# A decoder layer in float32: self-attention's product by V in sixteen squares of the array, the memory's weights on another queue, and a rearranged end

## The chip, the cores and the metric

The kernel runs on one core of a Trainium2 chip. A core has a matrix engine (TensorE, PE in the profile, with its weight loads shown as PEld), a vector engine (VectorE, DVE), an activation engine (ScalarE, ACT), a general engine (GpSimd, POOL), a synchronisation engine that only issues transfers (SyncE, SP), and 16 DMA engines. Each engine works through its own instruction stream in order and waits on semaphores. PE writes only to PSUM, eight banks of 128 partitions x 512 float32; DVE and ACT read PSUM, POOL does not. Transfers can be issued from SP, ACT and POOL.

The metric is the device time of one execution in microseconds. Times are compared with the median of runs of the kernel before.

## The reference

The input is x of 8 x 256 x 1024 (batch, token, channel), float32 throughout. Three blocks follow each other, each with a residual and a layer normalisation after it:

```python
x = layernorm(x + self_attention(x))        # 32 heads of 32, 8 key/value heads, rope, causal
x = layernorm(x + cross_attention(x, ctx))  # 32 heads of 128, 8 key/value heads, rope by position, key mask
x = layernorm(x + memory(x))                # 256 slots, the best 8, softmax, gate
```

What matters here is the first. Queries, keys and values are products of x with 1024 x 1024, 1024 x 256 and 1024 x 256 matrices; four query heads share one key/value head.

```python
attn = softmax(q @ k.T / sqrt(32) + causal)   # 256 x 256 for each head
out  = attn @ v                               # 256 x 32 for each head
return out.reshape(256, 1024) @ wo.T
```

The memory block projects each token to 64 channels, scores it against 256 slots, keeps the best eight, mixes their values, and adds the result with a gate that depends on the logarithm of the token's variance and on its mean over all tokens.

## The kernel before, in words

**Self-attention** (`self_attention`, about 0 to 1247 us) goes in 64 steps, s = 0 to 63, eight for each batch b; step c of a batch treats four query heads of four different key/value groups, c // 4 choosing which four. Inside this part the orders of PE and POOL are those in which the code names the instructions; the orders of DVE, ACT and SP are set by a planner. A step does:

- `transposed` (L295, L300), four times: the softmax weights of one head, 128 queries by 3 x 128 entries (the causal half has been left out), are transposed by PE in three 128 x 128 pieces into a bank of their own, `tr`, and copied to SBUF by ACT.
- `scores(s+1)` (L260): eight products on four 32-row strips of the array, into the two PSUM tiles `sc`. Then DVE adds the mask and takes the maximum (L275), ACT takes the exponential with its sum (L280), DVE the reciprocal (L284), and ACT scales (L286).
- `query(s+2)` (L207) with its rope on DVE (L217 to L220).
- `others(s)`: the output projection of the batch before (`project_out`, L340, L345, with the normalisation L134 to L146), or the keys and values of the next batch (L207, L233), and `turn` (L359), which transposes the normalised rows for cross-attention.
- `weighted(s)` (L308, L313): the product by V, eight products with 128 rows and 32 columns each, so that four heads lie side by side in four column strips of the array, and one copy by DVE (L318).

Between these, in steps 4 to 59, stand four products of cross-attention's keys and values (`one`, L677 and L683), part of a scheme that makes each 2 x 2 block product from seven products instead of eight (`seven`). Its sums of weights are made by POOL (`sum_event`, L385 to L434), one or two events in a step, and stored in DRAM.

Weights come through nine rotating SBUF buffers of 4 KB a partition, `w4` (`weights`, L110), loaded on SP's queue. SP runs ahead as far as these buffers are free. The key and value matrices `wk` and `wv` of self-attention are loaded once and stay.

**Cross-attention** (about 1250 to 3413 us) has 128 steps of one head for 512 queries: scores (L785), softmax (L794 to L805), a transposition of the weights in 32 x 32 blocks by DVE (`xa_turned`, L819), the product by V on four row strips of the array (`xa_weighted`, L836), four copies by ACT (L844), and query and output products (L683, L889) in between. V is read back from DRAM so that each strip has its copy (L602, on POOL's queue). Here only PE's order is written out. `memory_setup` stands at its beginning: it loads the memory block's weights on SP's queue (L1056 to L1065) and puts four empty places and then its preparations into the list `fill`, from which each step takes two entries.

**The tail** (`tail`, from about 3413 us) projects the last output, does the memory block for the last four of the 16 row tiles (`memory_tile`), and finishes all tiles (`final`): a product (L1312), the gated sum with row sums (L1315), the mean on DVE (L1321), the squares on ACT (L1323), the reciprocal root on POOL (L1324, L1325), one more DVE operation (L1326), and the normalisation by DVE for odd and by ACT for even tiles (L1330, L1332), stored by POOL's queue (L1333).

PSUM: three banks `mm` and one `tr` beside the two `sc` tiles of two banks each. In cross-attention two more single banks replace part of `sc`.

## Time and profile before

| | us |
|---|---|
| median of three runs (lowest, highest) | 3523.22 (3518.35, 3524.01) |
| the profiled execution | 3526.79 |
| its span, first to last instruction | 3524.6 |

The mean granted clock of the profiled execution is 0.985. In a row of the timeline the columns are the start in us from the span's beginning, the length in us, engine, line, operation, tiles (out<-in), shape and count. In the answer by stretch they are the stretch, its length, then busy us and number of instructions for PE, PEld, DVE, ACT and POOL, the clock that PE was granted, the busy share of the DMA engines and GB/s. In a row of waits they are who waited for whom, us in total, times, and the longest. Ends of matrix products are modelled and overlap the next start; how long PE is held is read from one start to the next.

### The profile page before, as it was taken

The numbers are of one execution on the slowest core, as the hardware profiler recorded it, in microseconds if no ns is written. First come the engines' busy times: TensorE is split into PE (matmuls) and PEld (weight loads), VectorE is DVE, ScalarE is ACT, GpSimd is POOL, SyncE is SP. The second block draws the span as 40 slices with busy tenths as digits, with TensorE's granted clock in tenths as the row PEclk, the third lists the DMA queues.
The fourth block names the chain that finished last, engine by engine and source line by source line (L and its number), as shares of the span: only waits on it lengthen the run. The fifth ranks groups of instructions, "written<-read, shape, count | busy, mean of one in ns | idle before, by whom it ended". The sixth has DMA issues, their size and how long they took to land.

```text
span 3524.6 us, 60801 instructions
## 1 busy us (share of the span) xinstructions
PE 3422.1 (97%) x22947; PEld 2472.4 (70%) x22947; DVE 2000.9 (57%) x5595; ACT 1287.0 (37%) x4139; POOL 1016.3 (29%) x1344
## 2 busy tenths in 40 slices
PE   7999999999999889999999999999999999999997
PEld 5777778777778657777676767766767776766763
DVE  3444444444444445655666566667566667566566
ACT  4544444444444423233323332323322333333224
POOL 3344555555656101211112111212111122111112
PEclk9999999999999999999999999999999999999997
DMA  6466777776766545444544444544444454444342
GB/s 246 165 212 210 260 251 235 242 244 211 261 230 213 170 149 172 142 127 144 162 142 147 136 131 133 162 143 149 137 132 127 152 162 134 142 130 133 132 150 96
DMA packets 233475, 600.52 MB, mean 170 GB/s; under 512 B 28832, under 2 KB 66016, under 8 KB 231904
## 3 DMA queue, kind: packets, MB, share of 16 engines
q1 hardware_dynamic: 159408, 411.32, 35.5%
q0 software_dynamic: 51712, 161.53, 13.7%
q10 hardware_dynamic: 22064, 23.79, 2.0%
q8 instruction: 183, 3.00, 0.3%
q14 instruction: 108, 0.88, 0.1%
HBM read 503.86 MB, written 92.67 MB: 169 GB/s over the span
## 4 chain that ended last, share of the span: by engine, by line
PE 90%; DVE 4%; ACT 2%; DMA 2%; issue 1%; POOL 1%; SPq 0%; POOLq 0%; ACTq 0%; DVEq 0%
PE mm L683 23%; PE mm L889 17%; PE mm L207 8%; PE mm L340 6%; PE mm L677 6%; PE sc L785 6%; PE mm L836 6%; PE tr L683 3%; PE tr L889 3%; PE tr L295 3%; PE mm L1165 2%; PE sc L260 2%; PE mm L233 1%; PE tr L836 1%; PE mm L308 1%
## 5 line engine op out<-in xcount | busy, mean ns | idle before, releaser
L683 PE MATMUL mm<-x1T,w 128*128 128x256 f32 x2976 | 712.8, 383 | 15.1 <-DMA w<-in_xa_wq 14.6
L683 PEld LDWEIGHTS mm<-x1T,w 128*128 128x128 f32 x2976 | 564.3, 191 | 169.3 <-issue 84.4
L799 ACT ACTIVATE xatt<-xatt,nmax 128x256 f32<-128x256 f32 x512 | 257.2, 503 | 499.6 <-DVE nmax L794 491.3
L889 PE MATMUL mm<-w,xoS 128*128 128x512 f32 x832 | 380.3, 596 | 0.9 <-issue 0.9
L602 POOL DMA_DIRECT2D v<-v x256 | 150.9, 596 | 739.2 <-PE mm L836 577.5
L300 ACT COPY at<-tr 128x384 f32<-128x384 f32 x253 | 121.1, 479 | 462.4 <-PE tr L295 462.4
L889 PE MATMUL mm<-w,xoT 128*128 128x512 f32 x620 | 284.1, 596 | 5.4 <-ACT xoT L844 4.1
L689 DVE TENSOR_TENSOR raw<-mm,half 128x256 f32<-128x256 f32 x339 | 141.6, 418 | 253.0 <-PE mm L683 154.7
L855 POOL TENSOR_TENSOR xoS<-xoT 128x512 f32<-128x512 f32 x62 | 79.1, 1276 | 700.1 <-ACT xoT L844 699.7
L689 DVE TENSOR_TENSOR half<-mm,half 128x256 f32<-128x256 f32 x256 | 107.3, 419 | 301.1 <-PE mm L683 249.8
L836 PEld LDWEIGHTS mm<-xat,v 32*128 32x128 f32 x6800 | 240.8, 186 | 42.5 <-issue 22.9
L889 PEld LDWEIGHTS mm<-w,xoS 128*128 128x128 f32 x832 | 154.9, 190 | 163.4 <-issue 144.2
L836 PE MATMUL mm<-xat,v 32*128 32x128 f32 x6800 | 265.8, 276 | 1.7 <-DVE rec L803 1.0
L785 PE MATMUL sc<-kT,qT 128*128 128x256 f32 x1024 | 264.2, 381 | 0.0
L805 ACT ACTIVATE xatt<-xatt,rec 128x256 f32<-128x256 f32 x512 | 231.0, 499 | 87.7 <-DVE rec L803 86.4
L280 ACT ACTIVATE att<-att,nmax 128x128 f32<-128x128 f32 (+1 forms) x512 | 225.5, 442 | 96.2 <-DVE nmax L275 96.2
L385 POOL TENSOR_TENSOR ws<-ws 128x256 f32<-128x256 f32 x320 | 240.8, 752 | 26.7 <-DMA ws<-in_xa_wk 6.2
L207 PE MATMUL mm<-xT,w 128*128 128x256 f32 x1024 | 245.6, 394 | 0.0
L844 ACT COPY xoT<-mm 128x128 f32<-128x128 f32 x425 | 88.9, 276 | 411.3 <-PE mm L836 287.3
L677 PE MATMUL mm<-w,ctxT 128*128 128x128 f32 x1792 | 224.6, 279 | 7.5 <-DMA w<-xa_wv_sums 3.1
L207 PEld LDWEIGHTS mm<-xT,w 128*128 128x128 f32 x1024 | 195.1, 196 | 48.4 <-issue 20.4
L340 PE MATMUL mm<-sa_wo,sa_oT 128*128 128x512 f32 x512 | 225.0, 592 | 0.0
(286 smaller groups left out, 5853.5 us busy)
## 6 DMA issues: line engine op xcount, KB each, us to landing
w<-xa_wq_sums SPq DMA_DIRECT2D x128, 512.0 KB, 3.6
w<-xa_wo_sums SPq DMA_DIRECT2D x124, 512.0 KB, 3.5
w<-in_xa_wo SPq DMA_DIRECT2D x97, 512.0 KB, 3.7
w<-in_sa_wq SPq DMA_DIRECT2D x64, 512.0 KB, 5.1
sa_wo<-in_sa_wo SPq DMA_DIRECT2D x64, 512.0 KB, 4.8
w<-in_xa_wq SPq DMA_DIRECT2D x64, 512.0 KB, 3.8
v<-v POOLq DMA_DIRECT2D x256, 128.0 KB
w<-xa_wk_sums SPq DMA_DIRECT2D x32, 512.0 KB, 7.0
```

The lines of the kernel that those rows point to most:

```text
L207: nc.tensor.matmul(ps[:, :S], lhsT=lhs[:, k, :], rhs=xT[:, k, :], start=(k == 0), stop=(k == KC - 1),)
L280: nc.scalar.activation(att[:, jj, lo:hi], att[:, jj, lo:hi], AF.Exp, bias=nmax[:, i : i + 1], scale=-1.0, accum_out=sums[:, i : i + 1],)
L340: nc.tensor.matmul(ps, lhsT=oTs[b * KC + c][:, tt * P : (tt + 1) * P], rhs=wos[b, half][c // 2][:, c % 2, :], start=(c == 0), stop=(c == K ...
L385: nc.gpsimd.tensor_tensor(out, in0, in1, op)
L677: nc.tensor.matmul(ps[:, t * P : (t + 1) * P], lhsT=rhs[:, k, t * P : (t + 1) * P], rhs=w[:, k, :], start=(k == 0), stop=(k == 3),)
L683: nc.tensor.matmul(ps[:, :S], lhsT=w[:, k, :], rhs=rhs[:, k, :], start=(k == 0), stop=(k == 3))
L689: nc.vector.tensor_tensor(out, in0, in1, ALU.add)
L785: nc.tensor.matmul(sc[:, qt, :], lhsT=qT[:, q0 : q0 + P], rhs=kT[:, b * S : (b + 1) * S], start=True, stop=True,)
L799: nc.scalar.activation(att[:, qt, :], att[:, qt, :], AF.Exp, bias=nmax[:, qt : qt + 1], scale=-1.0, accum_out=sums[:, qt : qt + 1],)
L805: nc.scalar.activation(att[:, qt, :], att[:, qt, :], AF.Identity, bias=0.0, scale=rec[:, qt : qt + 1])
L836: nc.tensor.matmul(banks[i][:, :P], lhsT=v[rows, c, :], rhs=at[rows, c, :], start=(c == 0), stop=(c == BLOCKS - 1),)
L889: nc.tensor.matmul(ps, lhsT=oT[lhs][:, u, off + p * P : off + (p + 1) * P], rhs=w[:, u, :], start=(u == 0), stop=(u == 1),)
```

## The change

1. **Product by V.** The transposes by PE and the product in four column strips go. After the softmax of a head DVE transposes it in 32 x 32 blocks into one tile `at` for two steps (even and odd s), and the product is made once for the two steps together: 104 products with 32 rows (keys) and 32 columns (channels of one head) each, on the sixteen 32 x 32 squares of the array. Each strip of 32 rows treats one block i of 32 queries out of each 128, against its own copy of V; the eight key blocks k follow one another and are summed in the strip's bank, one of four. The causal zeros are left out by block, so 40 of the 104 have 128 columns and 64 have 64. The product stands at the odd step, in two bursts, before the query and after the others. Its results lie in the two `sc` tiles. Four copies by ACT take them to SBUF.
2. **V by way of DRAM.** `values` stores V's rows in DRAM on ACT's queue, and `load_values` reads each half back four times, once for each strip, on SP's queue.
3. **Key and value weights** are no longer kept, but loaded for each batch through the `w4` buffers.
4. **Order.** Scores of odd steps come at the beginning of the step before them, those of even steps at the end, after the second burst. Query weights are asked for three steps ahead and output weights at steps 6 and 1 of a batch; the normalisation after the output projection is done one step later; the tables' transposes come at a step's end. The bank `tr` becomes a fourth `mm`. The `sc` tiles are given up one step later.
5. **Memory.** `memory_setup` runs at cross-attention's second step, its loads stand on POOL's queue, and two empty places remain of four. Tiles for the first query heads and the first softmax get their places early.
6. **End.** A scaling of the slot weights goes from DVE to ACT; the variance is written before the normalisation, and the last tiles' normalisation goes to ACT; two of the early `final` calls go to the end; in `final` the mean and the last factor go to POOL, the stores to SP's queue, and the last tile is normalised and stored in two halves.

```diff
-        self.banks = [(self.pool("mm", 3, space=PSUM), "mm")] * 3
-        self.banks_tr = [(self.pool("tr", 1, space=PSUM), "tr")]
+        self.banks = [(self.pool("mm", 4, space=PSUM), "mm")]
...
+        def load_kv(b, name):
+            for i in range(2):
+                src = a[name][:, :, i * P : (i + 1) * P] if name == "sa_wk" else a[name][:, 4 * i : 4 * i + 4, :]
+                wkvs[b, name, i] = self.weights([P, *src.shape[1:]], src)
...
-            nc.scalar.copy(vs[b][:, tt, :], ps[:, :256])
+            rows = sp.tile([P, SA_KV * SA_D], F32, name="sa_vrow", bufs=2)
+            nc.scalar.copy(rows, ps[:, :256])
+            if tt == 0:
+                v_d[b] = self.dram.tile([S, SA_KV * SA_D], F32, name=f"sa_v_{b}")
+            nc.scalar.dma_start(out=v_d[b][tt * P : (tt + 1) * P, :], in_=rows)
...
+            if s % 2 == 0:
+                ats[s // 2] = sp.tile([P, 4, 12, 2, 32], F32, name="at")
+            at = ats[s // 2]
...
+                for jj in range(2):
+                    turned = at[:, 2 * h + jj, :, s % 2, :]
+                    nc.vector.transpose(
+                        turned[:, :8].rearrange("p (c t) q -> p t c q", t=2),
+                        att[:, jj, :256].rearrange("p (t c q) -> p t c q", t=2, q=32),
+                    )
+                    nc.vector.transpose(turned[:, 8:], att[:, jj, 256:].rearrange("p (c q) -> p c q", q=32))
+
+        def load_values(b, half):
+            v = vs[b, half] = sp.tile([P, BLOCKS, 4 * SA_D], F32, name="sa_v", bufs=2)
+            rows = v_d[b].rearrange("(c i) d -> i c d", i=32)[:, :, half * P : (half + 1) * P]
+            for i in range(4):
+                nc.sync.dma_start(out=v[32 * i : 32 * i + 32], in_=rows)
...
+        def weighted(s, rest):
+            b, c = divmod(s, KC)
+            at, v = ats[s // 2], vs[b, c // 4]
+            if not rest:
+                pos[s] = [p_sc.tile([P, 2, 512], F32, name="sc") for _ in range(2)]
+            banks = [pos[s][i // 2][:, i % 2, :P] for i in range(4)]
+            for k in range(3, BLOCKS) if rest else range(3):
+                for i in range(max(k - 4, 0), 4):
+                    rows = slice(32 * i, 32 * i + 32)
+                    for j in range(4):
+                        lo, block = (0, slice(2 * k, 2 * k + 2)) if k <= i else (
+                            64, slice(2 * k + 1, 2 * k + 2) if k < 4 else slice(k + 4, k + 5)
+                        )
+                        nc.tensor.matmul(
+                            banks[i][32 * j : 32 * j + 32, lo:], lhsT=v[rows, k, 32 * j : 32 * j + 32],
+                            rhs=at[rows, j, block].rearrange("p x u q -> p (x u q)"),
+                            start=(k == 0), stop=(k == 4 + i),
+                        )
...
+            for i in range(4):
+                nc.scalar.copy(
+                    oT.rearrange("p u (t i q) -> p i t u q", t=2, i=4)[:, i],
+                    banks[i].rearrange("p (t u q) -> p t u q", t=2, u=2),
+                )
...
+            if s % 2:
+                weighted(s, False)
+            elif not first:
+                one()
+            if s % 2 == 0 and s + 1 < last:
+                scores(s + 1)
             if s + 2 < last:
                 query(s + 2)
+            while norms:
+                norms.pop(0)()
             for part in others(s):
                 part()
-            weighted(s, ats)
+            event()
+            one()
+            if s % 2:
+                weighted(s, True)
+                if s + 1 < last:
+                    scores(s + 1)
+            if c < 2:
+                load_values(b, c)
+            elif c == 6:
+                load_out(b, 0)
+            if b and c == 1:
+                load_out(b - 1, 1)
+            if s + 3 < last:
+                load_query(s + 3)
             while mine:
                 one()
...
-        self.memory_setup()
...
+            if H == 1:
+                self.memory_setup()
...
-            nc.sync.dma_start(out=t, in_=a[name] if src is None else src)
+            nc.gpsimd.dma_start(out=t, in_=a[name] if src is None else src)
...
-            nc.vector.tensor_scalar(w, w, rec, None, ALU.mult)
+            nc.scalar.activation(w, w, AF.Identity, bias=0.0, scale=rec)
...
-        nc.vector.tensor_scalar(nmean, sums[:, 0:1], sums[:, 1:2], -root / E, ALU.add, ALU.mult)
+        nc.gpsimd.tensor_tensor(nmean, sums[:, 0:1], sums[:, 1:2], ALU.add)
+        nc.gpsimd.tensor_scalar(nmean, nmean, -1.0 / E, None, ALU.mult)
...
-        nc.vector.scalar_tensor_tensor(nmr, nmean, 1.0 / root, rstd, ALU.mult, ALU.mult)
+        nc.gpsimd.tensor_tensor(nmr, nmean, rstd, ALU.mult)
...
-        finals(NT - 7)
+        finals(NT - 5)
```

## The prediction

> **What bounds the kernel now.** I read the shares of the engines first, then busy time by stretch, then TensorE's (PE's) timeline inside one step of self-attention, and its waits.
>
> ```profile
> PE 3422.1 (97%) x22947; PEld 2472.4 (70%) x22947; DVE 2000.9 (57%) x5595; ACT 1287.0 (37%) x4139; POOL 1016.3 (29%) x1344
> ```
>
> ```profile
> 480.00:640.00 160.00, 158.00 (x1033) 122.16 (x1032) 76.42 (x283) 76.19 (x254) 87.24 (x116) 1.00 0.73 243
> ...
> 1200.00:1240.00 40.00, 27.73 (x176) 20.22 (x173) 19.32 (x73) 21.68 (x76) 4.26 (x3) 0.80 0.65 232
> 1240.00:1320.00 80.00, 69.86 (x321) 47.24 (x323) 34.28 (x85) 18.47 (x57) 7.52 (x14) 0.92 0.43 132
> 1320.00:1760.00 440.00, 437.93 (x3180) 312.13 (x3176) 265.69 (x636) 141.27 (x467) 72.81 (x85) 1.00 0.46 150
> ...
> 3490.00:3525.00 35.00, 15.53 (x36) 6.52 (x35) 21.28 (x80) 18.80 (x29) 14.56 (x33) 0.63 0.47 190
> ```
>
> The columns after the length are PE, weight loads, DVE, ACT, POOL, the granted clock, the DMA share and GB/s. PE is full in self-attention (to about 1247) and in cross-attention (to about 3413). Only the joint between them (1200 to 1320) and the tail show gaps. So time is won by taking work off PE, or gaps out of the joint; work given to DVE is free as long as PE does not wait for it.
>
> Inside one step:
>
> ```profile
> 672.88 0.64 PE L308 MATMUL mm<-at,sa_v 128*32 128x256 f32 x8
> 673.33 0.40 PE L313 MATMUL mm<-at,sa_v 128*32 128x128 f32 x8
> 673.66 2.05 PE L677 MATMUL mm<-w,ctxT 128*128 128x128 f32 x16
> 675.55 0.49 PE L295 MATMUL tr<-ident,att 128*128 128x128 f32 x3
> 675.88 1.95 PE L677 MATMUL mm<-w,ctxT 128*128 128x128 f32 x16
> ...
> 1732.10 2.07 PE L836 MATMUL mm<-xat,v 32*128 32x128 f32 x64
> 1734.10 1.99 PE L683 MATMUL mm<-x1T,w 128*128 128x256 f32 x8
> ```
>
> Starts matter, since ends overlap. Three transposes hold PE from 675.55 to 675.88, 0.33 us; the product by V from 672.88 to 673.66, 0.78 us. The last two lines are cross-attention's product by V on four row strips, the nearest thing to the new one: 64 passes in 2.00 us.
>
> **The change, part by part.** The sum is made against the profiled execution, 3526.8 us (span 3524.6), which is 3.6 us over the median of 3523.2.
>
> *Work taken off PE.* Each of 64 steps loses four groups of transposes and one product: 4 x 0.33 + 0.78 = 2.10 us, in all -134 us. All of it is on the path.
>
> *The new product.* A pair of steps has 104 products in two bursts (48, then 56), each two passes in float32, like every product here (L836: 32 products, 64 passes): 208 passes. 40 products stream 128 columns and 64 stream 64. In L836's burst each strip starts a pass every 0.112 us (the timeline's rounds are 0.11 apart), the four strips of a round within 0.02 us, 6.7 ns apart. If sixteen squares run side by side as four strips do, a round of sixteen takes max(0.112, 16 x 6.7 ns) = 0.11 us a pass. First burst: three rounds of two passes, 0.67 us. Second burst: rounds of 16, 16, 12, 8 and 4 squares, 0.22 + 0.21 + 0.16 + 0.12 + 0.12 = 0.83 us. L836's 2.00 us is 16 x 0.112 = 1.79 plus 0.2 for turning the array over; I take 0.3 a burst since the first start also comes late. That is 2.1 us a pair, +67 us. Below: columns alone, (80 x 0.107 + 128 x 0.053)/16 = 0.96 us plus 0.4, +44. Above: nothing shows PE starting more than L836's 64 passes in 2.00 us over a whole burst; at 31 ns a pass, 208 take 6.5 us, +208. I take the low value, because L308 shows four column squares and L836 four row strips at that spacing, and L836's 31 ns is explained by its columns. A rule in the Trainium skill speaks against this: "TensorE: Matmul & The Clock Gate", section Back-to-back issue gap, gives a floor of about 25 ns between starts however few columns, and "TensorEngine Tiling (Array Packing)", section Instruction Overhead, warns against small dimensions for that reason. By it the bursts would be 208 x 25 ns + 0.6 = 5.8 us a pair, an estimate of +186 us; the starts 6.7 ns apart say that it does not hold between squares, but no run here shows sixteen.
>
> *The results share the scores' PSUM.* After the second burst the next scores wait until ACT has copied four 128x128 results:
>
> ```profile
> 1703.96 0.43 ACT L844 COPY xoT<-mm 128x128 f32<-128x128 f32 x2 [6.53 <-PE mm L836]
> 1704.28 0.28 ACT L844 COPY xoT<-tr 128x128 f32<-128x128 f32 x1
> 1704.43 0.30 ACT L844 COPY xoT<-mm 128x128 f32<-128x128 f32 x1
> ```
>
> There the last copy ends 0.86 us after PE's next work started (1703.87). In the new order the first strips end some 0.3 us before the last, and entering scores costs time anyway, so I take 0.4 us a pair, +13; bounds 0.2 and 1.2, +6 to +38.
>
> *Waits in self-attention.*
>
> ```profile
> PE tr L295 <- ACT at L300: 21.0, 32, 1.5
> PE mm L683 <- DMA w<-in_xa_wq: 13.1, 2, 9.9
> PE mm L295 <- ACT att L286: 6.2, 1, 6.2
> PE tr L295 <- ACT att L286: 3.9, 1, 3.9
> ```
>
> The first, third and fourth go with the transposes: -31. New: an odd step's first burst needs the whole softmax of scores issued in the step before. In the step of 682 scores end on PE at 683.26 and the last L286 at 690.36, 7.1 us later; the last head's DVE transposes add about 0.7. So 7.8 us must be covered. A step with four products of the next attention offers a query (3.65), three products (1.8 each) and an output projection (6.87) or keys or values (3.6): 12.6 to 15.9 us, enough. Steps without these products (0 to 3, 60 to 63) offer 2.6 to 7.3. I take 6 at step 61, 8 at 63 (DVE is held there by x1T's four 1024-wide operations), 3 at the start: +17. Net -14; bounds -25 and +5.
>
> *DVE* gets eight transposes a step. L819 gives 0.707 us for 128x512, and DVE's other 256- and 128-wide operations 0.42 and 0.28, so 4 x 0.70 = 2.8 us, less the removed 0.41 us copy (L318). Around 660 to 702.6 DVE is busy 19.5 of 42.6 us, 9.7 a step; then 12.1 of some 18.7, 65%. Cross-attention runs at 60% (265.7 of 440) with PE 99.5% busy, so I price it nearly at nothing. ACT loses four 0.48 us copies a step and gains two of 0.28.
>
> *DMA.* Key and value weights are fetched for every batch through the nine w4 buffers (+14.7 MB), V goes to DRAM by ACT's queue and comes back four times by SP's (+10.5 MB): 25 of 600 MB, with a share of 0.73 in the busiest stretch. Behind SP's wait for V stand query and product weights; a step of some 19 us between the write and its use covers it. Keys' weights in 512-byte rows may delay the start by 2 us. With DVE: +8; bounds 0 and +30. Deferred normalisations end a DVE wait for POOL that PE never felt: nothing. Output weights are asked for one or two steps earlier, and PE waits for none of them now (no row): nothing. Table transposes and POOL's sums change place inside a step; POOL is 55% busy there (87.2 of 160) and covers it.
>
> *The joint.* SP, in order, issues:
>
> ```profile
> 1286.22 0.65 SPq L1063 DMA_DIRECT2D m_in<-in_m_wu  x1
> ...
> 1299.05 0.49 SPq L1056 DMA_DIRECT2D m_gate_bias<-in_m_gate_bias  x1
> 1299.59 0.97 SPq L110 DMA_DIRECT2D w<-in_xa_wq  x2
> ```
>
> Query weights stand behind the memory's loads, and PE waits 9.95 us until 1306.16. On POOL's queue, a step later, they hold nothing that PE needs at once: -10. POOL's own V reloads (L602) stand behind twelve issues of 0.6 us, 7 us, with a pair of steps in hand. The router's turn comes after two empty places instead of four: if its weights are late, +4. Bounds -12 and +5.
>
> *The tail* is DVE's (26.8 of 30 us from 3460). It loses four scalings (0.35) and 32 one-column operations (about 0.15): -6; gains 1.5 normalisations (0.8), and two final tiles (1.4 each) move from DVE's idle time at 3453 to 3460 to the end: +4. POOL's longer chain per tile (five operations of 0.2 to 0.55) is shorter than DVE's 1.5 us and ACT's 1.3. Net -2; bounds -6 and +5. Other tile places and the order of banks (six in turn before and after): nothing, +-3.
>
> Sum: -134 + 67 + 13 - 14 + 8 - 10 - 2 = -72. 3526.8 - 72 = 3454.8; less 3.6, 3451 against the median.
>
> **Rivals.** *Slower: PE cannot start passes that fast.* At L836's 31 ns a pass the bursts cost 208 instead of 67: -72 + 141 = +69, 3592. It decides from the burst time where the -72 is gone: (67 + 72)/32 = 4.3 us a pair, 18 ns a pass after turning. For it: no sustained rate here is higher. Against: L836 is bound by columns.
>
> *Four at a time.* Squares of one strip, or of one column, take turns: (80 x 0.112 + 128 x 0.058)/4 + 0.6 = 4.7 us a pair, +150: -72 + 83 = +11, 3534. Against it: L308 streams four different right sides through the same rows.
>
> *The burst waits for DVE or ACT.* If in-order DVE holds the last blocks 1 us longer than covered, every pair pays 1 us, +32, 3483; 2 us, 3515. For it: where rope work came between, scores to last L286 took up to 9.4 us instead of 7.1, and DVE's load rises by a quarter. Against it: 4 to 8 us of cover in most steps.
>
> **How the numbers follow.** Forecast (3422 to 3475) 0.55; waits for DVE, ACT or DMA (3475 to 3515) 0.20; four at a time (3515 to 3545) 0.11; slow starts (over 3545) 0.10; better than 3422 0.04. A measurement tells 0.2%, 7 us, from no change. Slower takes 0.10 and 0.07 of the four-at-a-time case, same the other 0.04, faster 0.79. The range runs from 3422 to 3530 and leaves out about 0.2.
>
> **What the next profile would show.** Right: groups of form 32*32 with some 6650 passes, 2.1 us a pair in two bursts; no L295 or L300; idle under 0.5 us before the scores of even steps; DVE some 180 us busier; no 9.9 us wait for in_xa_wq; 625 MB moved. Wrong: bursts over 4 us, PE idle before first bursts in steady steps (released by DVE's transposes), or PE waiting for DMA of w or V.

## The result and the profile after

The changed kernel takes 3505.07 us in the median of five runs (3502.96 to 3509.42), the kernel before 3522.71 beside it (3518.35 to 3524.01): ratio 0.9958, 95% interval 0.9947 to 0.9969. The profiled execution took 3504.15 us, its span is 3502.4 against 3524.6. So the change is faster, by 18 us in the medians and 22 in the spans, where -72 was forecast. The time lies in the range, in the band of the rival "the burst waits for DVE or ACT" (3475 to 3515); whether it lies there for that reason is what the experiments were for.

The shares of the engines on the page of the changed kernel:

```profile
PE 3388.1 (97%) x27811; PEld 2459.2 (70%) x27811; DVE 2113.6 (60%) x5997; ACT 1201.2 (34%) x4030; POOL 1030.2 (29%) x1385
```

PE has 34 us less to do and 4864 passes more; DVE has 113 us more, not the 180 foreseen (the new transposes take 160, and the copy that goes, which the 180 left out, took 26), ACT 86 less. The stretches that answer to those shown of before:

```profile
480.00:640.00 160.00, 153.56 (x1610) 121.15 (x1610) 90.14 (x321) 58.51 (x217) 86.43 (x115) 0.96 0.76 255
1200.00:1240.00 40.00, 24.45 (x297) 17.49 (x298) 23.45 (x72) 14.55 (x54) 3.78 (x2) 0.79 0.55 197
1240.00:1320.00 80.00, 77.76 (x520) 55.53 (x519) 41.92 (x115) 25.41 (x82) 19.32 (x32) 1.00 0.59 190
1320.00:1760.00 440.00, 438.71 (x3067) 310.92 (x3066) 264.99 (x627) 136.75 (x451) 68.21 (x78) 1.00 0.47 147
3467.00:3502.00 35.00, 13.93 (x27) 5.34 (x26) 19.00 (x52) 17.75 (x28) 15.64 (x53) 0.64 0.47 187
```

In self-attention (first row) PE stands still for 6.4 of 160 us instead of 2.0, and the granted clock fell from 1.00 to 0.96. The joint (third row) is full now. The last 35 us have DVE busy for 19.0 us instead of 21.3, and POOL for a little more.

One step's timeline on PE:

```profile
646.19 1.49 PE L333 MATMUL sc<-at,sa_v 32*32 32x128 f32 x96
647.60 3.72 PE L208 MATMUL mm<-xT,w 128*128 128x256 f32 x16
651.16 7.03 PE L367 MATMUL mm<-sa_wo,sa_oT 128*128 128x512 f32 x16
658.03 1.89 PE L741 MATMUL mm<-ctxT,w 128*128 128x256 f32 x8
659.85 1.39 PE L333 MATMUL sc<-at,sa_v 32*32 32x64 f32 x112
661.34 1.35 PE L267 MATMUL sc<-sa_kT,sa_qT 32*128 32x128 f32 x16
```

From start to next start the two bursts (L333) hold PE for 1.41 and 1.49 us, 2.9 a pair instead of 2.1. And PE's waits up to 1320 us, the largest of them:

```profile
PE sc L333 <- DVE at L300: 18.5, 9, 12.4
PE mm L208 <- DMA xT<-in_xT: 10.2, 1, 10.2
PE sc L267 <- ACT sa_oT L343: 8.8, 8, 1.2
PE mm L735 <- DMA w<-xa_wv_sums: 7.8, 2, 5.8
PE sc L333 <- DMA sa_v<-sa_v: 6.1, 1, 6.1
PE mm L741 <- DMA w<-in_xa_wq: 3.8, 2, 1.9
PE mm L741 <- DMA w<-xa_wk_sums: 3.4, 1, 3.4
```

Where the 22 us of the spans lie, by the starts of the same work in both traces: cross-attention's first scores come at 1251.9 instead of 1268.1 (-16.2); from there to its first product by V 35.4 us instead of 47.7 (-12.3, the joint); to its last product by V 2099.8 instead of 2097.3 (+2.5); from there to the end 115.3 instead of 111.5 (+3.8). So the joint did what was said, the end a little worse, and nearly all that is missing, 44 us of the forecast's -60, is missing in self-attention.

### The profile page after: what moved, and what is told of

The parts are those of the page before. It is cut to its first block, busy times and chain, and to the rows that moved or that the text cites. A ratio compares the mean times of both kernels' runs of the same rounds, so it can differ in the third digit from the quotient of the medians.

```text
span 3502.4 us, 71117 instructions
## 1 busy us (share of the span) xinstructions
PE 3388.1 (97%) x27811; PEld 2459.2 (70%) x27811; DVE 2113.6 (60%) x5997; ACT 1201.2 (34%) x4030; POOL 1030.2 (29%) x1385
## 3 DMA queue, kind: packets, MB, share of 16 engines
q1 hardware_dynamic: 194672, 441.00, 38.6%
q8 instruction: 221, 3.62, 0.4%
## 4 chain that ended last, share of the span: by engine, by line
PE 71%; POOL 8%; issue 6%; DMA 6%; DVE 6%; ACT 2%; SPq 0%; POOLq 0%; ACTq 0%; DVEq 0%
PE mm L741 23%; PE mm L947 20%; PE mm L894 7%; PE sc L843 6%; PE mm L208 4%; POOL ws L417 3%; PE mm L735 3%; PE mm L367 2%; PE mm L1226 2%; DMA xa_wo_sums<-ws 2%; DMA xa_wq_sums<-ws 2%; PE sc L333 1%; PE sc L267 1%; POOL xa_wo_sums L466 1%; PE mm L1002 1%
## 5 line engine op out<-in xcount | busy, mean ns | idle before, releaser
L741 PE MATMUL mm<-x1T,w 128*128 128x256 f32 x3584 | 851.1, 381 | 5.0 <-DMA w<-in_xa_wq 3.8
L741 PEld LDWEIGHTS mm<-x1T,w 128*128 128x128 f32 x3584 | 676.3, 190 | 190.7 <-issue 87.7
L947 PE MATMUL mm<-w,xoS 128*128 128x512 f32 x992 | 449.2, 595 | 1.2 <-issue 1.2
L947 PE MATMUL mm<-w,xoT 128*128 128x512 f32 x744 | 338.2, 597 | 5.3 <-ACT xoT L902 4.1
L947 PEld LDWEIGHTS mm<-w,xoS 128*128 128x128 f32 x992 | 185.0, 190 | 194.2 <-issue 173.5
L208 PE MATMUL mm<-xT,w 128*128 128x256 f32 x1280 | 301.9, 392 | 10.2 <-DMA xT<-in_xT 10.2
L208 PEld LDWEIGHTS mm<-xT,w 128*128 128x128 f32 x1280 | 244.3, 195 | 59.9 <-issue 23.7
L747 DVE TENSOR_TENSOR raw<-mm,half 128x256 f32<-128x256 f32 x384 | 158.8, 414 | 153.0 <-PE mm L741 118.1
L947 PEld LDWEIGHTS mm<-w,xoT 128*128 128x128 f32 x744 | 138.7, 190 | 147.7 <-issue 126.8
L735 PEld LDWEIGHTS mm<-w,ctxT 128*128 128x128 f32 x1792 | 213.7, 197 | 24.9 <-issue 17.2
```

What stands on the lines that cost most here:

```text
L208: nc.tensor.matmul(ps[:, :S], lhsT=lhs[:, k, :], rhs=xT[:, k, :], start=(k == 0), stop=(k == KC - 1),)
L735: nc.tensor.matmul(ps[:, t * P : (t + 1) * P], lhsT=rhs[:, k, t * P : (t + 1) * P], rhs=w[:, k, :], start=(k == 0), stop=(k == 3),)
L741: nc.tensor.matmul(ps[:, :S], lhsT=w[:, k, :], rhs=rhs[:, k, :], start=(k == 0), stop=(k == 3))
L747: nc.vector.tensor_tensor(out, in0, in1, ALU.add)
L947: nc.tensor.matmul(ps, lhsT=oT[lhs][:, u, off + p * P : off + (p + 1) * P], rhs=w[:, u, :], start=(u == 0), stop=(u == 1),)
```

## The experiments

All runs are compared by their ratio to the kernel before on the same chip. A difference between two ratios, times 3522, is given in us; it is uncertain by some 6 us, so small effects are read from stages of the trace. "Alone" means one edit on the changed kernel.

### Every round of squares twice

```diff
-            for k in range(3, BLOCKS) if rest else range(3):
+            for rep, k in [(r, k) for k in (range(3, BLOCKS) if rest else range(3)) for r in range(2)]:
...
-                            start=(k == 0), stop=(k == 4 + i),
+                            start=(k == 0 and rep == 0), stop=(k == 4 + i and rep == 1),
```

> The changed kernel with every round of squares gone through twice: for each key block k the squares of all strips, then the same ones again, summed into the same bank. 208 more passes a pair of steps, 6656 in all; the output is not the layer's, since the product by V counts twice. It measures what a pass costs when nothing else is added. The prediction's size: rounds of sixteen at 0.11 us, so 1.5 us more a pair, +48 us over the changed kernel's 3505. My theory now (TensorE starts squares only every 11 to 12 ns once a burst has run for 32 passes, as read between starts in the trace after: 790 ns for 64 passes and 853 ns for 79): 208 x 10.8 to 12.3 ns = 2.25 to 2.56 us a pair, +72 to +82 us. Rival (self-attention is bound there by GpSimd's sums of weights or by the transfers, and TensorE's work is partly hidden): under +25 us.

3797.75 us, ratio 1.0781 (1.0764 to 1.0797): +290. PE's timeline of a pair without a pause inside:

```profile
660.74 2.73 PE L333 MATMUL sc<-at,sa_v 32*32 32x128 f32 x192
663.40 3.72 PE L208 MATMUL mm<-xT,w 128*128 128x256 f32 x16
...
675.70 2.58 PE L333 MATMUL sc<-at,sa_v 32*32 32x64 f32 x224
678.26 1.03 PE L267 MATMUL sc<-sa_kT,sa_qT 32*128 32x128 f32 x7
```

Thirteen first bursts and eight second ones without such a pause took 2.665 and 2.57 us on average, so 208 more passes cost 1.25 + 1.07 = 2.32 us, 11.1 ns each. That is what the trace after had said (2.25 to 2.56), +74 us for 32 pairs; 7.2 ns a pass, as forecast, falls, and so does the thought that PE's work is hidden there. The other 216 us no theory had. They are waits, most of them without a releaser (113 us more up to cross-attention's first scores), and a lower clock behind them (100 us; mean granted clock 0.951 instead of 0.982):

```profile
PE sc L333 <- issue: 126.2, 42, 4.9
```

### The 104 products in one burst

```diff
             if s % 2:
-                weighted(s, False)
-            elif not first:
+            if s % 2 == 0 and not first:
                 one()
...
             if s % 2:
+                weighted(s, False)
                 weighted(s, True)
```

> The changed kernel with the 104 products in one burst at the end of the odd step, where the second one stood, instead of two. Theory A (the bursts that come first wait for the softmax of the step before: the row of waits for DVE's transposes gives 18.5 us in nine times, 12.4 of them in the last step; and every burst pays once for turning over and filling): a turn of 0.25 us saved 32 times, -8, and 5 to 16 us of waits gone: -10 to -24 us, 3481 to 3495 us. Theory B (the waits come from work that is late anyway and turn up at the next place): -8 at most, and the last step's 12 us stay.

3580.76 us, ratio 1.0161 (1.0147 to 1.0175): +72, on the other side of both theories. The waits for the softmax did shrink (the row for DVE's transposes fell from 18.5 to 5.5 us), and a burst costs 2.80 us instead of 2.90. But there is the same new wait, 20 times in bursts and some times behind them, with a granted clock of 0.968:

```profile
PE sc L333 <- issue: 68.2, 20, 5.2
```

PE's timeline of this kernel:

```profile
648.47 2.70 PE L333 MATMUL sc<-at,sa_v 32*32 32x128 f32 x208
651.27 1.35 PE L267 MATMUL sc<-sa_kT,sa_qT 32*128 32x128 f32 x16
652.55 2.39 PE L734 MATMUL mm<-w,ctxT 128*128 128x128 f32 x19
657.47 5.02 PE L734 MATMUL mm<-w,ctxT 128*128 128x128 f32 x29 [2.54 <-issue]
```

PE stops in the middle of 48 like products whose weights and inputs are there. Its instructions are not: the answer on DMA traffic for 652 to 658 us of the same run has one packet of instructions,

```profile
q1 hardware_dynamic: 2077, 1.09, 87.4%
q0 software_dynamic: 154, 0.51, 25.0%
q8 instruction: 1, 0.02, 1.4%
```

and over the whole run 221 of them with 3.62 MB, 16 KB each. The 27,811 matrix instructions and as many weight loads are 252 to a packet, with PE's semaphore instructions 256.5; so they come in blocks of 256. In the trace's records this packet starts at 654.58 and takes 1.37 us; PE goes on 1.5 us after its end. Of the pauses of over 1.3 us between like instructions before 1290 us, 23 have this form: each ends with the same instruction of a block (numbers 193 and 194, modulo 256, semaphore instructions counted) and 1.25 to 1.6 us after a packet has landed. All 43 waits of over 1 us without a releaser in the doubled kernel's self-attention end with these two numbers too. A burst of 208 passes uses 416 instructions in 2.8 us, where products of 128 columns, 0.112 us from start to start, need 128 x 0.112 = 14.3 us for 256, and the next block isn't there in time. With bursts of 96 and 112 passes (192 and 224 instructions with their loads) and 12 us of other work between them, as in the timeline above, the kernel after has no pause of this form of over 1 us. The prediction took the two bursts for a matter of order; they are what keeps PE supplied.

### 128 columns everywhere

```diff
                         lo, block = (0, slice(2 * k, 2 * k + 2)) if k <= i else (
-                            64, slice(2 * k + 1, 2 * k + 2) if k < 4 else slice(k + 4, k + 5)
+                            0, slice(2 * k, 2 * k + 2) if k < 4 else slice(k + 3, k + 5)
```

> The changed kernel with 128 columns in all 104 products of a burst instead of 64 in 64 of them: the same number of instructions, 64 columns more in 128 of 208 passes. The extra columns take wrong blocks, so the output is not the layer's. If the number of instructions sets the rate: 128 passes of 0.11 us on sixteen squares are 7 ns each, under the 11 to 12 ns between starts, so nothing in the full rounds; the two short rounds at the end (8 and 4 squares, two passes each) grow by up to 0.2 us, 0 to +6 us over the changed kernel. If columns set it (64 columns at 0.055 us and 128 at 0.11, and the rate is set by squares waiting for one another): 128 x 0.055/16 = 0.44 us a pair at least, with the short rounds 0.6 to 1.0, +14 to +32 us.

3515.6 us, ratio 0.9980 (0.9968 to 0.9992): +8. First bursts kept their 1.415 us, though a quarter of their products have twice the columns now; second ones grew from 1.49 to 1.85. In the 1.49 are 0.10 us in which the scores behind the burst wait for the copies; the 1.85 have no such wait, so the burst itself grew by 0.46 us. That is over the 0.2 allowed where only instructions count, and at the lower end of the 0.44 to 1.0 where only columns do; the +8 us in all are under the 14 to 32 of that case, as the waits for the copies fell by 6 us. What tells most is the difference between the bursts: in each round of the first (one pass of all squares of a key block) some square had 128 columns already, in four of the five key blocks of the second none had. The longest square of a round counts, and it counts in full: eight rounds x 0.053 us = 0.43, against 0.46 measured.

### Four steps in one product

```diff
-            if s % 2 == 0:
-                ats[s // 2] = sp.tile([P, 4, 12, 2, 32], F32, name="at")
+            if s % 4 == 0:
+                ats[s // 4] = sp.tile([P, 4, 12, 4, 32], F32, name="at")
...
-                att = sp.tile([P, 2, 384], F32, name="att", bufs=3)
+                att = sp.tile([P, 2, 384], F32, name="att", bufs=2)
...
-            banks = [pos[s][i // 2][:, i % 2, :P] for i in range(4)]
+            banks = [pos[s][i // 2][:, i % 2, : 2 * P] for i in range(4)]
...
-            oT = sp.tile([P, 2, S], F32, name="sa_oT", bufs=6)
+            oT = sp.tile([P, 4, S], F32, name="sa_oT", bufs=2)
...
-            if s % 2:
+            if s % 4 == 3:
                 weighted(s, False)
...
```

> The changed kernel with the product by V made once for four steps instead of two: 104 products of 256 and 128 columns, so half the instructions for the same columns; one tile of transposed weights for four steps, the output of self-attention in tiles of four steps (two of them), and two buffers instead of three of the softmax weights, to make room. If the number of instructions costs the time: two bursts of 2.9 us become one of 40 x 2 x 0.215/16 + 128 x 11.5 ns + 0.8 = 1.07 + 1.47 + 0.8 = 3.3 us, so 2.5 us less for four steps, -40 us, and half of the 32 times 0.4 us before the scores that follow, -6: 3455 to 3470 us. If columns cost it: the bursts keep their sum, only turning and filling (0.3 + 0.3 us, 16 times) and those 6 us go, -15: 3485 to 3492 us. If something else bounds self-attention (GpSimd's sums, transfers): within 8 us of the changed kernel.

3481.28 us, ratio 0.9874 (0.9859 to 0.9889): -30, between the two cases. Bursts of four steps, in this kernel's timeline (from start to next start 2.05 us, and 2.02 for the second where the copies are not late):

```profile
663.92 2.12 PE L333 MATMUL sc<-at,sa_v 32*32 32x256 f32 x96
665.97 3.72 PE L208 MATMUL mm<-xT,w 128*128 128x256 f32 x16
...
678.27 1.92 PE L333 MATMUL sc<-at,sa_v 32*32 32x128 f32 x112
```

4.07 us for four steps instead of 5.81: 1.74 us x 16 = 28 us. The -30 is not these 28 alone. In the profiled execution self-attention became 38.6 us shorter (cross-attention's first scores at 1213.3 us instead of 1251.9), and cross-attention, whose code is the same, 23.7 us longer between its first and its last product by V: PE waits 27 us there instead of 13, mostly for VectorE, and the clock is lower behind these waits. Why VectorE comes later there is open.

With these bursts, nine kinds of burst are known, and one rule describes their lengths: **0.13 us for the burst, 6.7 ns for each pass, and for each round the time of its longest square (0.107 us for 128 columns, 0.053 for 64, 0.215 for 256), all added.**

| burst | passes | rounds x longest square | rule | measured |
|---|---|---|---|---|
| changed and wide, first | 96 | 6 x 0.107 | 1.41 | 1.42, 1.415 |
| changed, second | 112 | 2 x 0.107 + 8 x 0.053 | 1.52 | 1.49 |
| wide, second | 112 | 10 x 0.107 | 1.95 | 1.85 |
| four steps, first | 96 | 6 x 0.215 | 2.06 | 2.05 |
| four steps, second | 112 | 2 x 0.215 + 8 x 0.107 | 2.17 | 2.02 |
| single | 208 | 8 x 0.107 + 8 x 0.053 | 2.80 | 2.80 |
| doubled, first | 192 | 12 x 0.107 | 2.70 | 2.67 |
| doubled, second | 224 | 4 x 0.107 + 16 x 0.053 | 2.91 | 2.57 |

The 0.13 us are what the first bursts leave. These, with full rounds only, hold the rule within 0.04 us, and two differences give its parts apart: twice the columns cost six rounds 0.64 us (0.106 each), twice the passes 1.25. Second bursts, with rounds of 12, 8 and 4 squares too, come out up to 0.34 below it; the 1.49, 2.02 and 2.80 also hold 0.10 us of wait for the copies. So a round of sixteen takes 16 x 6.7 ns and 0.107 us one after the other, 0.21 us, not side by side, 0.11. It is a description of these lengths, not a mechanism, and the 6.7 ns are no spacing that one sees: in a first burst of the kernel after, starts are 6.7 ns apart inside the first two rounds of sixteen, and the last 63 starts are spread over 0.79 us, 12.8 ns apart on average. Each pass also has a weight load of its own, and no run changes the loads alone; whether they are what the passes cost is not tested.

### The order of the squares

```diff
-                for i in range(max(k - 4, 0), 4):
-                    rows = slice(32 * i, 32 * i + 32)
-                    for j in range(4):
+                for j in range(4):
+                    for i in range(max(k - 4, 0), 4):
+                        rows = slice(32 * i, 32 * i + 32)
```

> The changed kernel with the two inner loops of a burst exchanged: for each key block k the strips i run fastest and the heads j slowest, so that neighbouring products lie in different row strips instead of the same one. The bursts of four kernels (the changed one, the doubled, the wide, the one for four steps) fit 0.32 us + 6.7 ns a pass + the columns' time divided by sixteen, added and not overlapped. If that is the array's own law (each pass must be issued, and the columns come on top), the order means nothing: bursts of 1.42 and 1.49 us as before, within 5 us of 3505. If the sum comes from neighbours in one strip waiting for each other: down to the larger of the two parts, 2.1 us a pair instead of 2.9, -26 us. If the order is worse, because now neighbours share a column strip: over +10 us.

Ratio 0.9972 (0.9958 to 0.9986), +5, at the edge of what the first theory allowed. First bursts take 1.415 us as before, so it is not neighbours in one row strip that hold each other up. (The law named in the expectation, a sixteenth of the columns' time, was a first form of the rule above; the wide kernel's first burst decides for the longest square.) Second bursts with the wait behind them grew from 1.49 to 1.66 us, which is the 5 us; 0.24 of it instead of 0.10 is the scores' wait for the copies. Why the columns add to the 6.7 ns instead of running beside them stays open.

### x of later batches

Two runs. The first only named the transfer later in the code, and took x between the halves of the key weights at the start:

```diff
-        load_kv(0, "sa_wk")
+        load_kv(0, "sa_wk", (0,))
         load_x(0)
+        load_kv(0, "sa_wk", (1,))
...
-            if c == 6 and b + 2 < B:
-                load_x(b + 2)
...
+            if c == 0 and 0 < b < B - 2:
+                load_x(b + 2)
```

> The changed kernel with the order of transfers on SyncE's queue changed in two places. At the start x stands between the two halves of the key weights and not behind both; and from step 6 on, the x of the batch after next (1 MB, whose buffer comes free late) is asked for two steps later, behind the weights of that step. If head-of-line waiting on this queue makes the waits for weights before products of cross-attention's keys and values (the trace after has 3.4 and 5.8 us ones at 573 and 890, right behind an x transfer, and 21.9 us of such waits in all): 8 to 12 us less there, and the first projection 1 to 2 us earlier, 3492 to 3498 us. If the transfers as such are late (the DMA engines are 0.8 busy) the waits only move: within 4 us of 3505.

Ratio 0.9963 (0.9952 to 0.9973), +2. The first projection starts at 9.96 instead of 13.37 us, more than was expected, but at 225 us only 0.9 of these are left, and cross-attention's first scores come at 1251.3 instead of 1251.9: V's transfer and the first softmax are waited for next. The second edit did nothing, since SyncE's order is the planner's: x still went ahead of the weights. SyncE's timeline of this run:

```profile
568.70 0.34 SPq L162 DMA_DIRECT2D xT<-in_xT  x1
569.09 0.42 SPq L109 DMA_DIRECT2D w<-xa_wk_sums  x1
569.56 0.43 SPq L109 DMA_DIRECT2D w<-in_sa_wq  x1
```

The second run moved the transfer off the queue:

```diff
-            nc.sync.dma_start(out=xTs[b], in_=a["xT"][b])
+            (nc.gpsimd if b > 1 else nc.sync).dma_start(out=xTs[b], in_=a["xT"][b])
...
-            if c == 6 and b + 2 < B:
-                load_x(b + 2)
...
             if s + 3 < last:
                 load_query(s + 3)
+            if c == 6 and b + 2 < B:
+                load_x(b + 2)
```

> The changed kernel with the x of a later batch loaded on GpSimd's queue, at the end of step 6 of a batch, instead of on SyncE's, where it waits up to 32 us for its buffer with the weights behind it. (In the run that asked for x later, the transfer was still issued ahead of the weights, at 568.7, so that run told nothing of this.) If this queue's waiting makes the waits for weights before products: the 3.4 us at 573 and the 5.8 us at 890 go, and with the smaller ones 8 to 12 us, 3493 to 3497 us. If the transfers are late whatever the queue: within 4 us of 3505.

3494.83 us, ratio 0.9931 (0.9915 to 0.9946): -9.5. Up to cross-attention's first scores PE's waits before products, by the rows of waits, fell from 20.3 to 9.3 us. The waits of 500 to 920 us, in the run:

```profile
PE mm L701 <- DMA w<-in_xa_table,pos_u: 4.0, 3, 2.2
PE sc L267 <- ACT sa_oT L343: 3.6, 3, 1.2
PE mm L735 <- DMA w<-xa_wv_sums: 3.4, 1, 3.4
```

The 3.4 us for xa_wk_sums are gone, the 5.8 for xa_wv_sums are 3.4. On SyncE x had waited up to 32 us for its buffer with the weights behind it. It did so in the kernel before too (31.1 us at most) without such waits; there the nine shared buffers held no key and value weights. That this is why the stop hurts now is argued, not shown, and the next run, which takes the key weights out of these buffers and leaves the value weights in them, does not bear it out.

### Key weights kept in SBUF

```diff
-                att = sp.tile([P, 2, 384], F32, name="att", bufs=3)
+                att = sp.tile([P, 2, 384], F32, name="att", bufs=2)
...
-        load_kv(0, "sa_wk")
+        wk = sp.tile([P, 2, KC, P], F32, name="wk")
+        for i in range(2):
+            nc.sync.dma_start(out=wk[:, i], in_=a["sa_wk"][:, :, i * P : (i + 1) * P])
...
-            rope(kTs[b][:, i, :], project(wkvs.pop((b, "sa_wk", i)), xTs[b]))
+            rope(kTs[b][:, i, :], project(wk[:, i], xTs[b]))
```

> The changed kernel with the key weights of self-attention kept in SBUF again instead of loaded for each batch (8 KB, paid by two instead of three buffers of softmax weights); value weights still come for each batch. 7.3 MB less to move, and two tiles a batch less through the nine shared buffers. If the added transfers and the shared buffers cost what the prediction gave them (+8 us for them and VectorE): 3 to 8 us faster than the changed kernel, and fewer waits for weights before products. If they are hidden: within 3 us.

3506.61 us, ratio 0.9959 (0.9946 to 0.9973): nothing. The waits before products stay (21.5 us). The reload of the key weights is hidden; what hurt was one transfer's place in a queue. (One of three buffers of softmax weights paid for the room; a loss by that could hide a small gain.)

### The copies after a burst

Two runs. Shared between ScalarE and VectorE:

```diff
-                nc.scalar.copy(
+                (nc.vector.tensor_copy if i % 2 else nc.scalar.copy)(
                     oT.rearrange("p u (t i q) -> p i t u q", t=2, i=4)[:, i],
```

> The changed kernel with the four copies of a burst's result shared between ScalarE and VectorE, two each, instead of four on ScalarE. The scores that follow wait for them: TensorE's part for scores grew by 11.8 us, and 8.8 us more are listed as waits for these copies, against 13 us in the prediction. If the length of four copies is what is waited for: two are 0.35 us shorter, -6 to -11 us in all. If it is what stands in front of the copies on the engine (ScalarE's store of a normalised tile, seven times), the seven waits of 1.2 us stay, as two copies are still on ScalarE: -3 to -7 us by the others alone; VectorE's own queue may make it nothing.

3530.79 us, ratio 1.0032 (1.0020 to 1.0044): +26, slower than the kernel before. Nearly every burst now waits for VectorE, which has other work in its queue:

```profile
PE sc L267 <- DVE sa_oT L343: 31.4, 31, 4.1
```

The Trainium skill, "TensorEngine Tiling (Array Packing)", section PSUM Bottleneck, advises to use ScalarE and VectorE both for emptying PSUM. Here 128 copies by ScalarE alone cost 0.27 us each, and half of them on VectorE cost 26 us more: so it is less the copy than what stands before it. What does so on ScalarE is shown by the answer for the copies' line in the kernel after (idle time before it and its releaser):

```profile
  PE sc L333: 183.5, 25
  DVE res L377: 114.5, 7
```

Seven times ScalarE stands with the store of a normalised tile at its head, which waits for VectorE's normalisation (res, L377); the copies are behind it. The store on GpSimd's queue:

```diff
-                    nc.scalar.dma_start(out=self.x1[t], in_=x)
+                    nc.gpsimd.dma_start(out=self.x1[t], in_=x)
```

> The changed kernel with the store of a normalised tile after self-attention issued on GpSimd's queue instead of ScalarE's. In the trace after the four copies of the result stand behind this store on ScalarE once a batch, and it waits for VectorE's normalisation; TensorE then waits 1.2 us before the next scores, seven times. The prediction gave the deferred normalisation nothing. If that is the cause: these seven waits go, -8 us, 3495 to 3499 us. If the copies are late for another reason, or GpSimd's queue takes the wait over (its sums of weights stand behind the store then): within 3 us of 3505.

3509.06 us, ratio 0.9966 (0.9954 to 0.9979): +3. The seven waits are gone (the row of waits for the copies 8.8 to 0.4 us), so the cause of that wait is shown. But the time isn't: waits before the tables' transposes grew from 1.3 to 6.8 us and before products from 20.3 to 24.3. GpSimd, whose queue now has the store that waits for the normalisation, also gathers the tables' rows and makes the sums of weights; that this is the way the gain was lost is argued from these rows.

### The last step, and the end

```diff
-        nc.vector.tensor_tensor(xb["T1"], xb["T3"], xb["B11"], ALU.subtract)
-        nc.vector.tensor_tensor(xb["T2"], xb["B22"], xb["T1"], ALU.subtract)
+        v = nc.gpsimd if first else nc.vector
+        v.tensor_tensor(xb["T1"], xb["T3"], xb["B11"], ALU.subtract)
+        v.tensor_tensor(xb["T2"], xb["B22"], xb["T1"], ALU.subtract)
...
-        nc.vector.tensor_tensor(xb["T4"], xb["B21"], xb["T2"], ALU.subtract)
+        v.tensor_tensor(xb["T4"], xb["B21"], xb["T2"], ALU.subtract)
...
-        nc.gpsimd.tensor_tensor(nmean, sums[:, 0:1], sums[:, 1:2], ALU.add)
-        nc.gpsimd.tensor_scalar(nmean, nmean, -1.0 / E, None, ALU.mult)
+        nc.vector.tensor_scalar(nmean, sums[:, 0:1], sums[:, 1:2], -1.0 / E, ALU.add, ALU.mult)
...
-        nc.gpsimd.tensor_tensor(nmr, nmean, rstd, ALU.mult)
+        nc.vector.tensor_tensor(nmr, nmean, rstd, ALU.mult)
```

> The changed kernel with two small edits far from each other, to be read by stages. (1) The three subtractions of 1024 columns with which cross-attention's first blocks of rows begin go from VectorE to GpSimd; in the trace after they stand on VectorE in front of the last softmax's transposes, and TensorE waits 12.4 us for these at step 63. If VectorE's order is the cause, the wait shrinks to under 5 us and cross-attention's first product by V comes 6 to 10 us earlier (1277 to 1281 instead of 1287.3). If the wait is only the softmax's own length, or the blocks are needed as soon, it comes within 3 us of 1287. (2) In the last part the mean and the last factor of each tile go back to VectorE as one operation each, all else stays. If GpSimd's five small operations a tile are what made the end longer by 3.8 us, the stretch from the last output projection's start to the end of the program falls from 115.1 to 110 to 112 us; if the cause is the order of the normalisations or the two tiles moved to the end, it stays within 1 us. Both right: 3491 to 3497 us in all, against 3505.

3502.49 us, ratio 0.9949 (0.9929 to 0.9969), -3. By stages: the end takes 110.6 us instead of 115.3 (-4.7), so GpSimd's small operations are what had made it longer. At step 63 the wait fell from 12.4 to 6.7 us, but from the last scores to cross-attention's first scores only 3.5 us were won (47.7 to 44.2), and its first product by V came at 1285.8, not 1277 to 1281. VectorE's timeline shows what held the last transposes next, a wait for the key mask's transfer:

```profile
1212.30 1.58 DVE L680 TENSOR_SCALAR bias<-w 128x1024 f32<-128x1024 int32 x1 [2.93 <-DMA w<-in_mask]
```

### The joint undone

```diff
             self.load_values(0, b)
+        self.memory_setup()
...
-            if H == 1:
-                self.memory_setup()
...
-            nc.gpsimd.dma_start(out=t, in_=a[name] if src is None else src)
+            nc.sync.dma_start(out=t, in_=a[name] if src is None else src)
...
-            None, None, turn_router, diagonals, router_keys, rows,
+            None, None, None, None, turn_router, diagonals, router_keys, rows,
```

> The changed kernel with one part undone: the memory block's preparation back at cross-attention's very start, its twelve loads on SyncE's queue, and four empty places before its first work. The prediction's price of this part was 10 us, from a wait of 9.95 us for query weights; the traces give 12.3 us between first scores and first product by V of cross-attention. If the queue is the cause: 8 to 13 us slower than the changed kernel, with a wait of about 10 us for in_xa_wq back near 1270. If it was another edit (places of tiles, order of banks): within 3 us of the changed kernel.

3522.29 us, ratio 1.0000 (0.9989 to 1.0011), +15: without this part the change would have been worth nothing. From first scores to first product by V it is 47.6 us again, and the wait is back:

```profile
1294.69 2.90 PE L741 MATMUL mm<-x1T,w 128*128 128x256 f32 x6 [9.38 <-DMA w<-in_xa_wq]
```

### Together

Four steps, x on GpSimd's queue, the two edits of the last step and the end, and x between the halves of the key weights at the start:

> The edits that gave their stage back alone, together on the changed kernel: the product by V for four steps, x of later batches on GpSimd's queue, the subtractions of cross-attention's first blocks on GpSimd, the end's mean and last factor on VectorE, and x between the two halves of the key weights at the start. Alone against the changed kernel: four steps 0.0084 of the time before (-30 us), x 0.0027 (-10), the end -4.7 by its stage, the last step about -3.5, the start -2 at the most. If they add up: 3505 - 50 = 3455 us. If self-attention has a second bound close behind (GpSimd's sums, which carry x's issues and the subtractions now, or the transfers), as when the store on GpSimd's queue gave 9.5 us at the scores and lost it before tables and products: 3468 us or more, with more waits for sums of weights and for tables.

3442.27 us (3430.45 to 3445.04), ratio 0.9766 (0.9749 to 0.9783): by the ratios 68 us under the changed kernel, by the medians 63, and 13 to 18 more than the 50 of the parts. So no second bound stands close behind, and GpSimd carries its new work. In the profiled execution self-attention is 61.5 us shorter than in the changed kernel and the end 5.5, cross-attention 8.3 longer. The shares of this kernel:

```profile
PE 3354.1 (97%) x24483; PEld 2426.3 (70%) x24483; DVE 2114.5 (61%) x6026; ACT 1196.0 (35%) x3966; POOL 1030.5 (30%) x1346
```

PE's waits up to cross-attention's first scores (1190.4), by their rows, fell from 71.0 us to 45.8, those before products from 20.3 to 10.7. Four steps alone had raised these to 28.8, and the fall is 18 us instead of the 11 that x's place gave alone. The start's gain was lost again, as before: 9.64 us at the first projection, but the scores at 217.5 us of this kernel stand at 215.0 with four steps alone. The mask's operation was tried beside it:

```diff
         self.load_mask(0)
-        self.mask_bias()
...
+        self.mask_bias()
         for part in self.queries:
```

> The same as the combination, and VectorE's operation for cross-attention's key mask named after self-attention's last step instead of before it. In the run with the subtractions on GpSimd, VectorE stood 2.9 us before this operation, waiting for the mask's transfer, while the last softmax's transposes were behind it; TensorE still waited 6.7 us at step 63. If it is this wait: 3 to 5 us less in the stretch from the last scores to cross-attention's first scores than in the combination without it. If the softmax of the last step is simply that long (scores at 1205.7, last transposes at 1220): within 1.5 us.

Ratio 0.9782 (0.9769 to 0.9796), no better than without. From last scores to first scores 40.7 us instead of 42.5: between the two cases. The wait for the transposes fell from 4.3 to 3.1 us, the one for query weights before it rose from 4.3 to 5.8. What bounds this step in the end is not settled.

## Why the prediction was right and wrong

It was right in sign, in the joint, and in part of its mechanisms, and wrong in size. Its terms against the two profiled executions, in us up to cross-attention's first scores unless said. PE's time for a kind of work is taken from each start to the next, without the wait before the next, and counted by the granted clock of the moment (at half the clock a microsecond counts half); what that leaves out is the row of the clock.

| term | forecast | measured | from |
|---|---|---|---|
| transposes and old product gone | -134 | -149 | PE's time for them 97.3 + 51.7 |
| new bursts | +67 | +92 | PE's time for them 91.7; 32 x (1.42 + 1.49) with the waits behind them |
| PSUM shared with scores | +13 | +24 | PE's time for scores 55.1 to 68.3, and 11.0 of waits for the copies, short ones included |
| waits gone and new | -14 | -3 | 31.2 before transposes gone, 24.7 before bursts and 3.2 before scores new |
| DVE and DMA, the start | +8 | +10 | before products 12.4 to 20.3, start +3.6, tables 3.3 to 1.3 |
| clock | none | +9 | time lost at a lower clock 24.0 to 33.2 |
| other work of PE | none | +1 | 983.9 to 985.2 |
| joint | -10 | -12.3 | first scores to first product by V |
| cross-attention | 0 | +2.5 | first to last product by V |
| end | -2 | +3.8 | last product by V to the end |

The rows add up to the 22 us of the spans. The first row was better than forecast by 15: three transposes held PE for 0.33 us in most places, but for 0.42 in a quarter of them, and for 0.5 where twelve follow one another. The next three rows lost 47 us.

**The step that failed** is in the second row: "If sixteen squares run side by side as four strips do, a round of sixteen takes max(0.112, 16 x 6.7 ns) = 0.11 us a pass." By the lengths of the bursts the two parts add: a full round takes 0.21 us. In the doubled kernel a pass costs 11.1 ns instead of the 7.2 that this step gives (1.50 us for 208). With the rule's 0.26 us for turning over instead of 0.6 (-11 us in all), the rounds take 2.64 of the measured 2.90 us a pair instead of 1.5 (+36): +25, the difference of the table's second row. The spacing of 6.7 ns is found inside the first two rounds of a burst, and not behind them. What misled was the row that it was read from: in L836's burst, 64 passes on four strips, 16 x (4 x 6.7 ns + 0.107) = 2.14 us would be more than the 2.00 measured, so there the parts do overlap. On sixteen squares they don't, and no row of before could say so. The bound of 4.3 us a pair that the first rival named as the break-even was not reached, and both "slow starts" (31 ns) and "four at a time" (4.7 us a pair) fell.

The Trainium skill, "TensorE: Matmul & The Clock Gate", section Back-to-back issue gap, has a floor of about 25 ns between starts; by that figure 5.8 us a pair is an estimate from below. The starts of this trace lie closer, 2.9 us a pair in all; the measured 2.9 is 0.8 from the forecast and 2.9 from this estimate. That small products are dear was true in kind: with twice the columns in each, the bursts took 28 us less.

**PSUM**: the term was 0.4 us a pair, and PE's scores do take 0.4 us more, 13 us in all. The missing 11 us are waits for the copies: one of 1.2 us a batch, and 0.10 behind most other bursts. The sentence that failed is "Deferred normalisations end a DVE wait for POOL that PE never felt: nothing." With the normalisation its store on ScalarE's queue was deferred, to a place in front of the copies. What is queued behind a moved instruction was asked for POOL and SyncE, but not for ScalarE.

**Waits**: 31 us went as forecast, but 28 new ones came instead of 17. Step 63 cost 13.7 us instead of 8, for the reason given (the operations on x1T stand before the last transposes on VectorE), the first two bursts 7.5 instead of 3, most of it one wait of 6.1 for V, step 61 3.5 instead of 6; 3.2 before scores had no price. The rival "the burst waits for DVE or ACT", whose band holds the time, is not what happened: between 95 and 1180 us no burst waited as much as 0.15 us, and the bursts' length is PE's own. That the time lies in that band is chance.

**DMA**: +10, near the price, but not for the reason given. Keeping the key weights gained nothing; x's transfer at the head of SyncE's queue cost 9.5. "Behind SP's wait for V stand query and product weights" looked at the wrong wait of that queue. The start was +3.6 instead of +2, and it hardly mattered, as 2.5 of the 3.4 us that another order gained were lost again by 225 us.

**End**: "POOL's longer chain per tile ... is shorter than DVE's 1.5 us and ACT's 1.3" compared the engines' busy times. The tiles do not overlap that well: VectorE stood 1.2 to 2.6 us before four of its last five normalisations, waiting for GpSimd's result. With two operations back on VectorE the stage lost 4.7 us.

**Clock**: no term was given. Up to cross-attention's first scores the trace after grants half the clock 14 times, for 3.4 to 17.1 us at a time, and in the 7 us before each of these times PE had stood still for 0.7 to 3.6 us. So a wait can cost more than its length: the doubled kernel has 113 us more of waits than the changed one and lost 100 us more at the lower clock, the kernel with one burst 47 and 45.

## What to carry to other kernels

A rate read where one limit covers another says nothing of the case in which both are near: measure a burst's passes and columns apart, and when they add, make each instruction larger (four steps instead of two: half the instructions, 28 us less in the bursts). When an instruction moves, look at what follows it on every queue that it touches; three of the surprises here, x on SyncE, a store on ScalarE, the mask on VectorE, were in-order engines standing with something unready at their head. And a dense burst has to leave PE's instruction supply time to refill.

## What was not expected of the hardware

PE's instructions arrive in blocks of 16 KB, 256 instructions (221 packets, 3.62 MB); with 208 passes in one piece PE ran into the end of a block 23 times, in the burst or behind it, and stood 1.3 to 5.2 us, until 1.25 to 1.6 us after the next block had landed. Rounds of sixteen squares have the length of 6.7 ns a pass and the longest square's time on top, whichever strip comes next. And the time to issue a transfer was not its own alone: that of x at the start took SyncE 0.41 us in the kernel before, behind one transfer of whole key weights, 0.64 behind one half of them in 512-byte rows, and 1.42 behind both.
